# A layer of two attentions and a feed-forward: groups turned four steps ahead, feed-forward stores in two halves

## The chip, the cores and the metric

One core of a Trainium2 chip. The metric is the device time of one launch in microseconds (us); a time is the median over runs. A core has TensorE (PE, matrix products; PEld are its weight loads), VectorE (DVE), ScalarE (ACT), GpSimd (POOL), and SyncE (SP), which here only issues DMAs. Each engine takes its instructions in order and waits at semaphores for the others.

## The reference

The input x is (2, 256, 128, 128): batch, time, bands, channels, in float32. Three residual parts follow each other:

```python
xt = _ln(x, ln_t_w, ln_t_b).transpose(0, 2, 1, 3)
x = x + _mha(xt, t_wi, t_bi, t_wo, t_bo, H_T, cm).transpose(0, 2, 1, 3)   # over time, causal
xf = _ln(x, ln_f_w, ln_f_b)
x = x + _mha(xf, f_wi, f_bi, f_wo, f_bo, H_F, bm)                          # over bands, |i - j| <= 16
xn = _ln(x, ln_n_w, ln_n_b)
h = jax.nn.gelu(xn @ w1.T + b1, approximate=False)                         # 128 -> 512
x = x + (h @ w2.T + b2)                                                    # 512 -> 128
```

`_ln` is a layer norm over the channels, `_mha` an attention with four heads of 32 channels.

## The kernel before

**Groups and steps.** The work is cut into groups of 512 tokens (four tiles of 128). First come 128 groups of attention over time (`OverTime`). Then come 16 runs; a run covers 32 times of one batch and has eight groups of attention over bands (`OverBands`) and then the eight feed-forward groups of the same tokens (`FeedForward`). The loop over `n` in `BoundedPath.run` (line 1343) has one step for each group; a step does parts of several groups, so that every engine has work. In this text the band steps of a run are B1 to B8 and the feed steps F1 to F8, and a group is named like the step with its number. F1 is the step at which the code's `turn` is true.

**Order.** Every engine is wrapped in `InOrder` (line 963), which pins each instruction to the place at which the program issues it. The order of the code in `run` is thus the order on each engine. All pinned instructions carry the helper's line, L973, in the profile, so they are told apart by their tiles.

**What a group goes through.** `statistics` (line 406) takes the mean and variance on VectorE: four BN_STATS and four BN_AGGR, tiles `stats` and `mv`. `root` (line 423) makes 1/sqrt(variance + eps) on GpSimd with two instructions, tile `rstd`. `normalize` (line 457) writes `xh` on VectorE with four instructions. `turn` (line 474) transposes it in 32x32 blocks on VectorE (tile `z`) and writes it with four DMAs to a buffer in DRAM (`turned`, a pool of three). `fetch` (line 486) reads it back with one DMA as `xnT`, channels on partitions, which TensorE multiplies. The fetch of group n + 2 is issued in step n, ahead of the turn of that step.

**A band step** on VectorE: one operation that adds the band mask to the scores of the fourth head (`bank<-bank,band`), the turn of a later group, three operations that divide (`bank<-bank,r`, `u`, `oT`), and the residual sum (`x<-bank,x`). ScalarE takes exponentials into `pf`. For the other three heads GpSimd sets the weights outside the band to zero with two AFFINE_SELECTs each, six masks in a step (`first_mask`, line 843). TensorE then sums the masked weights with a matrix of ones (`sums`, line 857: `bank<-pf,ones`, one product for each head) and weighs the values (`bank<-pf,v`). The sums of a band group come in the step after its masks; those of B8 come in F1. In F1 VectorE inverts the sums of B8 by a reciprocal.

**A feed step** on TensorE: `hidden` multiplies `xnT` by w1 in four parts (`bank<-xnT,w1f`), ScalarE applies the gelu into `hT`, and `bank<-w2T_sb,hT` multiplies by w2. `divide` (line 951) adds the result on VectorE into `res` and calls `store` (line 1103), which at each second group issues four DMAs of 128 KB for the pair. `res` is a pool of two buffers of four groups each.

**How far ahead.** `turn_ahead(n)` (line 1370) normalizes and turns group n + 3. `statistics_of_feed(n)` (line 1366) takes the statistics and the root of feed group n + 4, late in step n, unless it is one of the first three of its run; those three (`early`, line 1364) are taken at the start of step n, right behind the masks of that step (line 1388). `late` (line 1449) issues the load of group n + 14, behind the turn.

Of the kernel before, what the change touches and what calls it, by code (L numbers as in the profile page):

```python
# [25 lines left out]
NT = 4  # L26
# [343 lines left out]
class Group:  # L370
# [32 lines left out]
    def bias(self):  # L403
        pass
# [147 lines left out]
    def divide(self):  # L552
        pass
# [127 lines left out]
def rows_of(h):  # L681
    return slice(h * D, (h + 1) * D)
# [9 lines left out]
class OverTime(Attention):  # L692
# [5 lines left out]
    early, late = (1, 2), (0, 3)  # L698
# [179 lines left out]

class FeedForward(Group):
    last = False  # L880

    def bias(self):
        path = self.path
# [67 lines left out]
    def divide(self):  # L951
        if self.last:
            for i in range(NT):
                dst = self.dst()[:, i]
                self.path.vector.tensor_tensor(dst, self.zps[i], dst, ALU.add)
                self.path.store_column(i)
        else:
            self.path.vector.tensor_tensor(self.dst(), self.zp, self.dst(), ALU.add)
            self.give("zp")
        self.store()  # L960


class InOrder:
# [14 lines left out]
class BoundedPath:  # L978
# [72 lines left out]
    def groups(self, x, out):  # L1051
        nc, k = self.nc, self.k
        B, T, FB, C = x.shape
        NC_T = T // P
        for b in range(B):
            for f0 in range(0, FB, GA):
                held = {}


                def load(g, f0=f0, b=b, held=held):  # L1060
                    if b == f0 == 0:
                        held["x"] = k.x0
                        return
                    if "x" not in held:
                        self.input_quad(held)
                    f = f0 + g // NC_T * NT
                    self.sync.dma_start(held["x"][rows_of(g)], self.of_times(x[b], g, slice(f, f + NT)))

                def store(g, f0=f0, b=b, held=held):
                    for i in range(NT if g % 2 else 0):  # L1070
                        f = f0 + i // NC_T * NT + g
                        self.sync.dma_start(
                            self.of_times(k.x1[b], i, slice(f - 1, f + 1)), held["res"][rows_of(i), :, g - 1 : g + 1]
                        )

                def part(name, g, i=None, a=0, held=held):
                    if name == "res" and name not in held:
                        self.quad(held, "res", 2)
                    if name == "x" and name not in held:
                        self.input_quad(held)  # L1080
                    if i is not None:
                        return self.longer(held[name], i * NT + g, a)
                    return held[name][:, :, g]

                for g in range(NT):
                    yield OverTime(self, partial(part, "x", g), partial(part, "res", g), partial(load, g), partial(store, g))
        for b in range(B):
            for r0 in range(0, T, RUN):
                run = []
                for t0 in range(r0, r0 + RUN, GB):  # L1090
                    held = {}


                    def load(g, t0=t0, b=b, held=held):
                        if g == 0:
                            self.input_quad(held)
                            self.quad(held, "x2", 2 * RUN // GB)
                        self.sync.dma_start(
                            held["x"][rows_of(g)].rearrange("q g t c -> q (g t) c"),
                            self.of_bands(k.x1[b], t0 + NT * g, NT),  # L1100
                        )

                    def store(g, t0=t0, b=b, held=held):
                        last = b == B - 1 and t0 == T - GB
                        n = 1 if last and g > 1 else 2
                        if last and g == NT - 1:
                            return
                        for i in range(NT if (g + 1) % n == 0 else 0):
                            self.sync.dma_start(
                                self.of_bands(out[b], t0 + NT * i + g + 1 - n, n),  # L1110
                                held["res"][rows_of(i), g + 1 - n : g + 1].rearrange("q g t c -> q (g t) c"),
                            )

                    def store_column(m, t0=t0, b=b, held=held):
                        to = out[b][t0 : t0 + GB].rearrange("(i g) (m q) c -> g m i q c", g=NT, q=D)
                        queue = self.scalar if m % 2 else self.sync
                        queue.dma_start(to[NT - 1, m], held["res"][:, NT - 1, m])

                    self.store_column = store_column

                    def part(name, g, i=None, a=0, held=held):
                        if name == "res" and name not in held:
                            self.quad(held, "res", 2)
                        if i is not None:
                            return self.longer(held[name], g * NT + i, a)
                        return held[name][:, g]

                    run += [(g, part, load, store) for g in range(NT)]
                for g, part, load, _ in run:
                    yield OverBands(self, partial(part, "x", g), partial(part, "x2", g), partial(load, g))  # L1130
                for g, part, _, store in run:
                    yield FeedForward(self, partial(part, "x2", g), partial(part, "res", g), None, partial(store, g))
# [210 lines left out]
    def run(self, x, out):  # L1343
        groups = list(self.groups(x, out))

        def do(n, *names):
            if 0 <= n < len(groups):
                for name in names:
                    getattr(groups[n], name)()

        def at(n, kind):
            return 0 <= n < len(groups) and isinstance(groups[n], kind)

        def do_at(n, kind, *names):
            if at(n, kind):
                do(n, *names)
# [7 lines left out]
        early = [i for i in range(3, len(groups)) if at(i, FeedForward) and at(i - 3, OverBands)]  # L1364

        def statistics_of_feed(n):
            if at(n + 4, FeedForward) and n + 4 not in early:
                do(n + 4, "statistics", "root")

        def turn_ahead(n):  # L1370
            do_at(n + 3, (OverBands, FeedForward), "normalize", "turn")

        groups[-1].last = True

# [3 lines left out]
        for n in range(len(groups) + 2):  # L1378
            feeds = [at(n - 2 + i, FeedForward) for i in range(5)]
            bands = [at(n - 2 + i, OverBands) for i in range(5)]  # L1380
            turn = feeds[2] and bands[1]
# [3 lines left out]
            if n == run0[0]:  # L1385
                self.free.sort(key=lambda i: i == self.banks["b2"])
            do(n, "first_half", "first_function", "first_mask")
            if n + 4 in early:
                do(n + 4, "statistics", "root")
            if n == 0:  # L1390
                do(3, "normalize_flat")
# [4 lines left out]
            if old is not None or new is not None:  # L1396
                time_scores(old, new)
                b = self.banks
# [48 lines left out]
            if n == 5:  # L1447
                k.late_weights()
            def late(n=n):
                do(n + 14, "load")  # L1450

            ahead = at(n, (OverBands, FeedForward))
# [3 lines left out]
            if not turn:  # L1456
                turn_ahead(n)
            if n != 1:
                do_at(n + 4, OverTime, "normalize", "turn")
            if ahead and not turn:  # L1460
                late()
# [9 lines left out]
            if not bands[2] and not turn:  # L1471
                statistics_of_feed(n)
# [26 lines left out]
            if turn:  # L1499
                turn_ahead(n)  # L1500
                late()
# [4 lines left out]
            if bands[2] or turn:  # L1506
                statistics_of_feed(n)
# [108 lines left out]
```

## Time and profile before

| what | us |
|---|---|
| median of 3 runs (2622.3 to 2624.03) | 2622.48 |
| the profiled execution, its own time | 2624.33 |
| its span, first to last instruction | 2622.3 |
| TensorE busy | 2611.9 (100%) |
| VectorE busy | 2136.2 (81%) |
| GpSimd busy | 1956.2 (75%) |
| ScalarE busy | 1824.6 (70%) |
| DMA queue 1, share of 16 engines | 50.3% |

The granted TensorE clock is 0.999 of full speed. The page gives busy time for each engine, the chain of work that ended last, and groups of equal instructions. The timeline lists instructions in order of time: start, length, engine, line, operation, out<-in, count, and in brackets the idle time before it with what ended it. The view by windows gives, for each stretch, its length and then the busy time of PE, PEld, DVE, ACT and POOL, each with the number of instructions. Ends of matmuls are modelled, so a busy TensorE is not by itself TensorE at its peak.

### The profile page before, as it was taken

The numbers are of one execution on the slowest core, as the hardware profiler recorded it, in microseconds if no ns is written. First come the engines' busy times: TensorE is split into PE (matmuls) and PEld (weight loads), VectorE is DVE, ScalarE is ACT, GpSimd is POOL, SyncE is SP. The second block draws the span as 40 slices with busy tenths as digits, with TensorE's granted clock in tenths as the row PEclk, the third lists the DMA queues.
The fourth block names the chain that finished last, engine by engine and source line by source line (L and its number), as shares of the span: only waits on it lengthen the run. The fifth ranks groups of instructions, "written<-read, shape, count | busy, mean of one in ns | idle before, by whom it ended". The sixth has DMA issues, their size and how long they took to land.

```text
span 2622.3 us, 156624 instructions
## 1 busy us (share of the span) xinstructions
PE 2611.9 (100%) x68688; PEld 1766.0 (67%) x68688; DVE 2136.2 (81%) x6410; ACT 1824.6 (70%) x3543; POOL 1956.2 (75%) x2311
## 2 busy tenths in 40 slices
PE   9999999999999999999999999999999999999999
PEld 6666666666666667666666666666666666766666
DVE  8888888888888897977878779788787797887974
ACT  7989998999899875564655746647557466475563
POOL 7999999999999987666667666665776666656762
PEclk9999999999999999999999999999999999999999
DMA  6656555565565544455455445454554444545543
GB/s 156 166 148 159 147 153 151 150 157 147 151 153 152 127 120 124 121 124 126 116 127 129 119 121 126 119 129 111 130 128 119 125 118 124 131 111 128 128 100 89
DMA packets 469798, 344.99 MB, mean 132 GB/s; under 512 B 43120, under 2 KB 404464, under 8 KB 469104
## 3 DMA queue, kind: packets, MB, share of 16 engines
q1 hardware_dynamic: 468408, 334.41, 50.3%
q8 instruction: 541, 8.86, 1.5%
q14 instruction: 153, 1.25, 0.2%
q10 hardware_dynamic: 696, 0.46, 0.1%
HBM read 167.98 MB, written 166.72 MB: 128 GB/s over the span
## 4 chain that ended last, share of the span: by engine, by line
PE 99%; DVE 0%; DMA 0%; ACT 0%; issue 0%; ACTq 0%; DVEq 0%
PE bank L973 99%; DMA x<-in_x 0%; ACT pf L973 0%; DVE stats L973 0%; DVE xnT L973 0%; ACTq L973 0%; ACT p L973 0%; DVE xh L973 0%; DVE vy L973 0%; ACT lnv L973 0%; DVE res L973 0%; DVE mv L973 0%; ACT root L973 0%; DVE rstd L973 0%; DVEq L973 0%
## 5 line engine op out<-in xcount | busy, mean ns | idle before, releaser
L973 ACT ACTIVATE hT<-bank,b 128x512 f32<-128x512 f32 x512 | 346.9, 688 | 522.5 <-PE bank L973 497.8
L973 POOL TENSOR_SCALAR_AFFINE_SELECT pf<-pf 128x512 f32<-128x512 f32 x768 | 476.6, 635 | 242.2 <-ACT pf L973 215.8
L973 PEld LDWEIGHTS bank<-w2T_sb,hT 128*32 128x32 f32 x16384 | 465.6, 110 | 137.4 <-issue 114.6
L973 PE MATMUL bank<-xnT,wf 128*32 128x512 f32 x4096 | 510.5, 593 | 1.2 <-ACT pf L973 0.7
L973 PE MATMUL bank<-xnT,w1f 128*32 128x512 f32 x4096 | 500.9, 592 | 0.0
L973 PE MATMUL bank<-w2T_sb,hT 128*32 128x128 f32 x16384 | 500.7, 273 | 0.0
L973 ACT ACTIVATE p<-bank 128x512 f32<-128x512 f32 (+1 forms) x1024 | 430.3, 495 | 63.5 <-PE bank L973 63.5
L973 DVE TENSOR_SCALAR xh<-x,mv,rstd 128x160 f32<-128x160 f32 (+1 forms) x1012 | 393.8, 432 | 35.9 <-POOL rstd L973 25.6
L973 POOL TENSOR_SCALAR_AFFINE_SELECT p<-p 128x1024 f32<-128x1024 f32 (+2 forms) x384 | 363.7, 947 | 57.3 <-ACT p L973 49.0
L973 PEld LDWEIGHTS bank<-wf,xnT 128*32 128x32 f32 x8192 | 237.5, 110 | 150.1 <-issue 91.0
L973 POOL TENSOR_TENSOR p<-p,p 128x512 f32<-128x512 f32 x256 | 323.7, 1286 | 10.7
L973 DVE BATCH_NORM_STATS2 stats<-x 128x6 f32<-128x128 f32 x1536 | 328.9, 277 | 3.1 <-DMA x<-in_x 3.1
L973 DVE TENSOR_TENSOR res<-bank,res 128x512 f32<-128x512 f32 (+1 forms) x259 | 171.0, 661 | 191.3 <-PE bank L973 163.3
L973 PE MATMUL bank<-qT,kT 32*64 32x80 f32 (+4 forms) x16384 | 303.7, 271 | 0.8 <-issue 0.7
L973 PEld LDWEIGHTS bank<-qT,kT 32*64 32x64 f32 x16384 | 260.6, 131 | 52.9 <-ACT kT L973 50.6
L973 ACT ACTIVATE pf<-bank 128x512 f32<-128x512 f32 x512 | 264.4, 603 | 35.1 <-PE bank L973 34.7
L973 DVE STREAM_TRANSPOSE z<-xh 128x512 f32<-128x512 f32 x380 | 270.4, 712 | 13.3
L973 POOL TENSOR_SCALAR rstd<-mv 128x4 f32<-128x4 f32 x251 | 57.3, 228 | 296.6 <-DVE mv L973 295.5
L973 PE MATMUL bank<-wn,oT 128*32 128x128 f32 x8192 | 276.3, 274 | 0.1
L973 POOL TENSOR_TENSOR rstd<-rstd,mhalf 128x4 f32<-128x4 f32 x251 | 260.6, 1038 | 20.9
L973 PE MATMUL bank<-wf,xnT 128*32 128x128 f32 x8192 | 272.9, 273 | 0.0
L973 DVE TENSOR_TENSOR bank<-bank,r 128x512 f32<-128x512 f32 x240 | 165.9, 691 | 108.0 <-PE bank L973 80.4
(100 smaller groups left out, 3746.2 us busy)
## 6 DMA issues: line engine op xcount, KB each, us to landing
turned<-z SPq DMA_DIRECT2D x1520, 64.0 KB, 2.6
xnT<-turned SPq DMA_DIRECT2D x380, 256.0 KB, 3.3
x<-res SPq DMA_DIRECT2D x256, 128.0 KB, 2.5
x<-x SPq DMA_DIRECT2D x128, 256.0 KB, 3.7
out<-res SPq DMA_DIRECT2D x252, 128.0 KB, 2.3
x<-in_x SPq DMA_DIRECT2D x124, 256.0 KB, 4.4
x<-in_x SPq DMA_DIRECT2D x4, 128.0 KB, 3.2
x<-in_x SPq DMA_DIRECT2D x6, 64.0 KB, 2.6
```

Source lines behind the costliest of these rows:

```text
L973: return self.tc.keep_in_program_order(emit(*args, **kwargs))
```

## The change

**Turned four steps ahead.** `turn_ahead(n)` turns group n + 4. The statistics move with it: `statistics_of_feed(n)` takes group n + 5, but not in the last band step, B8; the first three of a run are taken at the start of steps n with n + 5 among them; and F5's are taken at the start of F1. The fetch stays where it was.

**Stores in two halves.** `store` issues the first two of the four DMAs of a pair and returns the other two, which `late` issues a step later, behind that step's turn and ahead of its load. The last four groups of all are stored as before.

```diff
@@ class FeedForward, divide
-        self.store()
+        self.others = self.store()
+
+    def store_others(self):
+        if self.others is not None:
+            self.others()
@@ store of a feed group
-                        for i in range(NT if (g + 1) % n == 0 else 0):
-                            self.sync.dma_start(
-                                self.of_bands(out[b], t0 + NT * i + g + 1 - n, n),
-                                held["res"][rows_of(i), g + 1 - n : g + 1].rearrange("q g t c -> q (g t) c"),
-                            )
+                        if (g + 1) % n:
+                            return
+
+                        def some(rows):
+                            for i in rows:
+                                self.sync.dma_start(
+                                    self.of_bands(out[b], t0 + NT * i + g + 1 - n, n),
+                                    held["res"][rows_of(i), g + 1 - n : g + 1].rearrange("q g t c -> q (g t) c"),
+                                )
+
+                        some(range(NT if last else NT // 2))
+                        if not last:
+                            return partial(some, range(NT // 2, NT))
@@ run
         def statistics_of_feed(n):
-            if at(n + 4, FeedForward) and n + 4 not in early:
-                do(n + 4, "statistics", "root")
+            if n + 5 not in early and not (at(n, OverBands) and at(n + 1, FeedForward)):
+                do_at(n + 5, FeedForward, "statistics", "root")
 
         def turn_ahead(n):
-            do_at(n + 3, (OverBands, FeedForward), "normalize", "turn")
+            do_at(n + 4, (OverBands, FeedForward), "normalize", "turn")
@@ run, at the start of a step, behind first_mask
-            if n + 4 in early:
+            if n + 5 in early:
+                do(n + 5, "statistics", "root")
+            if turn:
                 do(n + 4, "statistics", "root")
@@ run, late
             def late(n=n):
+                do_at(n - 2, FeedForward, "store_others")
                 do(n + 14, "load")
```

The order of TensorE and of ScalarE, and the banks that they use, are the same in both kernels. On GpSimd, where the band steps of a run end, this stood before (`pf<-pf` are the masks, six for a step; a pair of `rstd` rows is a root):

```order
L973 AFFINE_SELECT pf<-pf 128x512 x30
L973 TENSOR_SCALAR rstd<-mv 128x4
L973 TENSOR_TENSOR rstd<-rstd,mhalf 128x4
L973 AFFINE_SELECT pf<-pf 128x512 x6
L973 TENSOR_SCALAR rstd<-mv 128x4
L973 TENSOR_TENSOR rstd<-rstd,mhalf 128x4
L973 AFFINE_SELECT pf<-pf 128x512 x6
L973 TENSOR_SCALAR rstd<-mv 128x4
L973 TENSOR_TENSOR rstd<-rstd,mhalf 128x4
L973 AFFINE_SELECT pf<-pf 128x512 x6
L973 TENSOR_SCALAR rstd<-mv 128x4
L973 TENSOR_TENSOR rstd<-rstd,mhalf 128x4
```

The x30 are the masks of B1 to B5, and the last x6 those of B8; the root behind these is that of F4. Now, at the same place:

```order
L978 TENSOR_SCALAR rstd<-mv 128x4
L978 TENSOR_TENSOR rstd<-rstd,mhalf 128x4
L978 AFFINE_SELECT pf<-pf 128x512 x6
L978 TENSOR_SCALAR rstd<-mv 128x4
L978 TENSOR_TENSOR rstd<-rstd,mhalf 128x4
L978 AFFINE_SELECT pf<-pf 128x512 x6
L978 TENSOR_SCALAR rstd<-mv 128x4
L978 TENSOR_TENSOR rstd<-rstd,mhalf 128x4
L978 AFFINE_SELECT pf<-pf 128x512 x6
L978 TENSOR_SCALAR rstd<-mv 128x4
L978 TENSOR_TENSOR rstd<-rstd,mhalf 128x4
L978 AFFINE_SELECT pf<-pf 128x512 x6
```

These are the roots of F1 to F4, each ahead of the masks of B5 to B8 (line L978 is the helper's new number). The root of F4 has moved from behind the masks of B8 to ahead of them.

VectorE from the start of B8 to the reciprocal in F1, before (`bank<-bank,band` opens a band step):

```order
L973 SCALAR_TENSOR_TENSOR bank_115<-bank_115,band 128x512
L973 TENSOR_SCALAR xh<-x_22992,mv,rstd 128x5x32 x4
L973 STREAM_TRANSPOSE z<-xh 128x512
L973 TENSOR_TENSOR bank_109<-bank_109,r_25856 128x512
L973 TENSOR_TENSOR x_23573<-bank_110,x_23573 128x512
L973 SCALAR_TENSOR_TENSOR u<-bank_109,r_25856 128x512
L973 TENSOR_TENSOR oT<-bank_114,u 128x4x4x32
L973 BN_STATS stats<-x_22992 128x6 x4
L973 BN_AGGR mv<-stats 128x2 x4
L973 RECIPROCAL ln<-bank_115 128x512
```

And now, from the end of B7:

```order
L978 BN_STATS stats<-x_23004 128x6 x4
L978 BN_AGGR mv<-stats 128x2 x4
L978 SCALAR_TENSOR_TENSOR bank_115<-bank_115,band 128x512
L978 TENSOR_SCALAR xh<-x_23004,mv,rstd 128x5x32 x4
L978 STREAM_TRANSPOSE z<-xh 128x512
L978 TENSOR_TENSOR bank_109<-bank_109,r_25881 128x512
L978 TENSOR_TENSOR x_23585<-bank_110,x_23585 128x512
L978 SCALAR_TENSOR_TENSOR u<-bank_109,r_25881 128x512
L978 TENSOR_TENSOR oT<-bank_114,u 128x4x4x32
L978 BN_STATS stats<-x_23585 128x6 x4
L978 BN_AGGR mv<-stats 128x2 x4
L978 RECIPROCAL ln<-bank_115 128x512
```

The statistics of F4 stand a step earlier, at the end of B7, and those of F5 stand where F4's were. The turn of B8 (`xh`, `z`) is now that of F4 instead of F3.

SP, in feed steps, before (`turned<-z` are the four writes of a turn):

```order
L973 DMA xnT<-turned 128x512
L973 DMA turned<-z 32x4x128 x4
L973 DMA out<-res 32x8x128 x4
L973 DMA xnT<-turned 128x512
L973 DMA turned<-z 32x4x128 x4
```

And now:

```order
L978 DMA xnT<-turned 128x512
L978 DMA turned<-z 32x4x128 x4
L978 DMA out<-res 32x8x128 x2
L978 DMA xnT<-turned 128x512
L978 DMA turned<-z 32x4x128 x4
L978 DMA out<-res 32x8x128 x2
```

Two of the four stores have moved behind the next step's turn; a `turned` row now writes the group of one step later.

More of the change, by code (lines that the diff above doesn't have):

```diff
@@ L880 @@
     last = False
+    others = None
     def bias(self):
```

## Prediction

> **What bounds the kernel now.** I read the page first, then TensorE's waits, then the span cut at the runs, then the timeline of one change from band steps to feed steps. A run is 8 band steps (B1 to B8) and 8 feed steps (F1 to F8); there are 16.
>
> ```profile
> span 2622.3 us, 156624 instructions
> ...
> PE 2611.9 (100%) x68688; PEld 1766.0 (67%) x68688; DVE 2136.2 (81%) x6410; ACT 1824.6 (70%) x3543; POOL 1956.2 (75%) x2311
> ...
> PE 99%; DVE 0%; DMA 0%; ACT 0%; issue 0%; ACTq 0%; DVEq 0%
> ```
> TensorE (PE) is busy almost without a break, and the chain that ended last is TensorE for 99%. Its waits:
>
> ```profile
> PE bank L973 <- POOL ident masks.py:199: 1.5, 1, 1.5
> PE bank L973 <- issue: 1.0, 4, 0.3
> PE bank L973 <- ACT pf L973: 0.7, 1, 0.7
> ```
> No DMA is among them, so none waited for a turned tile. A busy row alone could hide slack, so here is the span from the first feed step of the first run to that of the last, and three runs of it (length, then PE busy):
>
> ```profile
> 972.21:2557.05 1584.84, 1583.24 (x41291) 1055.87 (x41287) 1279.14 (x3857) 940.00 (x1569) 1049.79 (x1444) 1.00 0.49 122
> 1396.00:1501.26 105.26, 105.26 (x2761) 69.72 (x2757) 84.76 (x257) 62.58 (x105) 69.86 (x97) 1.00 0.49 122
> 1501.26:1606.51 105.25, 105.25 (x2761) 69.54 (x2756) 84.88 (x257) 62.48 (x105) 69.79 (x97) 1.00 0.50 125
> 1606.51:1712.65 106.14, 105.45 (x2761) 69.45 (x2756) 84.99 (x257) 62.59 (x105) 69.78 (x97) 1.00 0.47 121
> ```
> ```profile
> 1684.33 1.58 ACT pf L973 x3
> ```
> Undisturbed runs agree to 0.01 us. The third holds the chain's one long piece off TensorE, and is 0.89 longer: a wait of TensorE is not made up later. 15 runs at 105.25 are 1578.75; the stretch took 1584.84, so 6.09 us of scattered waits is all that better timing could return there. So each edit is worth what it adds to or takes from TensorE's waits.
>
> **The change part by part.** *Turned a step earlier.* The four DMAs that write a turned tile go out a step sooner, so the fetch of xnT, behind them on SP's queue, no longer stands waiting for their landing:
>
> ```profile
> SPq L973 <- DMA turned<-z: 416.0, 465, 3.7
> ```
> ```profile
> xnT<-turned SPq DMA_DIRECT2D x380, 256.0 KB, 3.3
> ```
> ```profile
> 1184.43 0.34 SPq L973 DMA_DIRECT2D xnT<-turned  x1
> ...
> 1190.55 1.90 PE L973 MATMUL bank<-xnT,w1f 128*32 128x512 f32 x16
> ```
> These 416 us are SP's own. The tile of F2 is fetched at 1184.43, lands some 3.3 later and is used at 1190.55: 2.8 to spare. Up to a step (6.1) more makes it some 9. Since TensorE never waited for a fetch, the gain is 0; the cover is needed less, not more.
>
> *Stores in halves.* 252 stores stay 252 issues of 128 KB; half are issued a step later, behind the turned tile and ahead of the next load. Nobody computes with what they write, and the result buffers are a pair, each reused a run later. I take 0, bounded below by the 6.09 above if spread stores should also quiet the scattered waits, and above by 0, since the fetches they could delay now have a step more.
>
> *Statistics a step earlier.* Counts stay the same on VectorE (DVE) and GpSimd (POOL); places change where bands turn into feed. Before, the statistics of F1, F2, F3 stand early in B5, B6, B7 and those of F4 late in B8. Now F1 to F3 stand early in B4 to B6, F4 late in B7, none in B8, and F5 early in F1. Each is followed on GpSimd by its root. GpSimd keeps the program's order, so the root of F4 now stands ahead of the six masks of B8, where before it came behind them. GpSimd there, before:
>
> ```profile
> 1176.44 3.93 POOL L973 TENSOR_SCALAR_AFFINE_SELECT pf<-pf 128x512 f32<-128x512 f32 x6 [0.97 <-ACT pf L973]
> 1180.35 0.23 POOL L973 TENSOR_SCALAR rstd<-mv 128x4 f32<-128x4 f32 x1
> 1180.66 1.04 POOL L973 TENSOR_TENSOR rstd<-rstd,mhalf 128x4 f32<-128x4 f32 x1
> 1182.67 3.93 POOL L973 TENSOR_SCALAR_AFFINE_SELECT pf<-pf 128x512 f32<-128x512 f32 x6 [0.97 <-ACT pf L973]
> 1189.25 0.23 POOL L973 TENSOR_SCALAR rstd<-mv 128x4 f32<-128x4 f32 x1 [2.65 <-DVE mv L973]
> ```
> The masks of B8 run from 1182.67 to 1186.60, gated by ScalarE. Now they wait for the root, the root for the mean and variance (mv), and those come late in VectorE's step:
>
> ```profile
> 1157.23 0.70 DVE L973 SCALAR_TENSOR_TENSOR bank<-bank,band 128x512 f32<-128x512 f32 x1 [0.50 <-PE bank L973]
> 1163.45 0.70 DVE L973 SCALAR_TENSOR_TENSOR bank<-bank,band 128x512 f32<-128x512 f32 x1 [0.50 <-PE bank L973]
> ...
> 1169.86 0.69 DVE L973 SCALAR_TENSOR_TENSOR bank<-bank,band 128x512 f32<-128x512 f32 x1
> ...
> 1176.26 0.69 DVE L973 SCALAR_TENSOR_TENSOR bank<-bank,band 128x512 f32<-128x512 f32 x1
> ...
> 1182.65 0.69 DVE L973 SCALAR_TENSOR_TENSOR bank<-bank,band 128x512 f32<-128x512 f32 x1
> 1183.25 1.60 DVE L973 TENSOR_SCALAR xh<-x,mv,rstd 128x160 f32<-128x160 f32 x4
> ...
> 1188.02 0.86 DVE L973 BATCH_NORM_STATS2 stats<-x 128x6 f32<-128x128 f32 x4
> 1188.79 0.36 DVE L973 BATCH_NORM_AGGREGATE mv<-stats 128x2 f32<-128x6 f32 x4
> ```
> The first five open B4 to B8; the turn of B8 begins at 1183.25. B4 waited for TensorE, so it starts at 1157.23 as before. A step with statistics takes 6.40 without a wait (1169.86 to 1176.26), so B5, B6, B7 open at 1163.63, 1170.03, 1176.43. B7 then has the form that B8 has now: 5.37 from 1182.65 to the late statistics at 1188.02. So those of F4 start at 1181.80 and end 1.13 later (1188.79 + 0.36 - 1188.02), at 1182.93. GpSimd answered 0.10 after such an end (1189.15 to 1189.25): 1183.03. The root takes 1.35 (1180.35 to 1181.70), the masks 3.93: from 1184.38 to 1188.31, 1.7 later than before. Who needs them:
>
> ```profile
> 1187.52 0.13 PEld L973 LDWEIGHTS bank<-pf,ones 128*32 128x32 f32 x4 [0.30 <-issue]
> 1187.95 1.04 PE L973 MATMUL bank<-pf,ones 128*32 128x512 f32 x8
> ```
> The sums over B8's weights stand in F1 and ran at 1187.95; three of their four heads wait for GpSimd, the third for the last mask. Before, 1.35 us lay between; now 0.36 are missing. The restart after a release has one row near it:
>
> ```profile
> 1180.25 0.59 ACT L973 COPY kT<-bank 128x512 f32<-128x512 f32 x1 [0.69 <-PE bank L973]
> ...
> 1180.99 0.81 PEld L973 LDWEIGHTS bank<-qT,kT 32*64 32x64 f32 x64 [0.20 <-ACT kT L973]
> ```
> 0.15 from 1180.84 to 1180.99. So the wait is 0.36 to 0.51 a run; I take 0.45, nearer the end that has a restart in it. TensorE keeps its order, so what is queued behind the sums waits too: the weighing of B8, the output of B7 and F2's first products, ready or not.
>
> The 3.93 of the masks is a span; the row behind starts 3.91 after the first. The Trainium skill (Perfetto Trace Analysis, GPSIMD Engine Instruction) says that such spans are unreliable and that the spacing of starts should be used. By that the sum is 0.02 a run less, 0.3 us in all; here the two hardly differ.
>
> *Behind it on VectorE.* The turn in B8, now of F4, waits for that root until about 1184.4, where it began at 1183.25: 1.2 later. From there to F1's reciprocal VectorE has as many operations as before (F5's statistics in the place of F4's), so it runs about 1.2 later into F1. The next that TensorE takes from it, by order of the banks, is B8's output bank:
>
> ```profile
> 1204.77 0.66 DVE L973 TENSOR_TENSOR x<-bank,x 128x512 f32<-128x512 f32 x1
> ...
> 1207.00 1.93 PE L973 MATMUL bank<-w2T_sb,hT 128*32 128x128 f32 x64
> ```
> Emptied at 1205.43, used at 1207.00: 1.57 covers 1.2, and TensorE is itself 0.45 later. Cost 0.
>
> **The sum.** 16 runs times 0.45 is 7.2 us (4.8 to 8.2 for 0.30 to 0.51, the lower end with 0.06 for small errors in eight added rows). The profiled execution took 2624.33, its span and 2.03 around it: with the change 2631.5. The median shown, 2622.48, is 1.85 below that execution; against it, 2629.7.
>
> **The rivals.** *The masks come in time* (not slower): were the root done 0.15 to 0.4 sooner, because VectorE is quicker out of B4 to B7 than its rows or the restart is shorter, 0 to 0.3 a run is left: 2622.5 to 2627.3. It decides at 0.33 a run, that is 5.2 us. For it: I add eight rows and miss by only 0.36. Against: VectorE stood saturated in the same form before, with steps of 6.39 to 6.41.
>
> *TensorE has slack.* The weight loads are 67% busy; if TensorE idled inside its rows, work behind the sums could be done faster and the delay swallowed: 2622.5. Against it stand the runs of 105.25 and the wait that lengthened one. The Trainium skill (Perfetto Trace Analysis, Identifying the Most-Contended Engine) says matmul busy time is a poor measure of distance to the roof and sends the reader to load time, which by its figure here would leave a third of the span free; the run lengths do not bear that out.
>
> *Faster.* Earlier fetches and halved stores thin out the scattered waits. At most 6.09 comes back, 2616.4, and only with no new wait; the waits that carry a name carry no DMA.
>
> *A second wait.* If VectorE is later into F1 than 2.0, the bank at 1207.00 is late as well. A further 0.4 a run gives 2636.
>
> That the change doesn't take place is excluded: the order shows the moved rows.
>
> **How the numbers follow.** The wait as worked out: 0.56, 2629.7 (own range 2627.3 to 2631.5). Masks in time: 0.32. Slack: 0.04. Faster: 0.05. Second wait: 0.03. A measurement of this kernel can tell about 0.2%, 5.2 us, from no change. Slower by more than that: 0.56 + 0.03 = 0.59; within: 0.32 + 0.04 = 0.36; faster: 0.05. The range reaches down through the cases without a wait, less the executions' own spread of some 1 us, and up to 0.51 a run with 2 us for scattered waits: 2621.5 to 2633.0.
>
> **What would show it.** In the changed profile: GpSimd's masks of B8 start some 1.7 later, right behind a root; TensorE waits once a run, at the sums in F1, for GpSimd's pf, 16 times; undisturbed runs take 105.7, not 105.25; SP's wait for turned tiles is nearly gone. I am wrong if runs stay at 105.25, or if TensorE's wait stands elsewhere.

## The result, and the profile after

The changed kernel takes 2629.84 us (median of 22 runs, 2626.89 to 2634.11), the kernel before 2622.64 us (22 runs beside them): 7.2 us more, a ratio of 1.0027 with a 95% interval of 1.0021 to 1.0032. The profiled execution of the changed kernel took 2629.27 us, 4.9 us more than that of before; its span is 2627.5 us, 5.2 more.

Three parts of the changed kernel's page: the span, the busy times, the chain that ended last by engine and by line.

```profile
span 2627.5 us, 156484 instructions
...
PE 2617.1 (100%) x68688; PEld 1862.0 (71%) x68688; DVE 2130.3 (81%) x6410; ACT 1825.3 (69%) x3543; POOL 1956.3 (74%) x2311
...
PE 98%; POOL 1%; DVE 0%; DMA 0%; issue 0%; ACT 0%; ACTq 0%; DVEq 0%
```

GpSimd (POOL) has entered the chain with 1%. All its pieces there lie between 944 and 978 us, in the first run; what the other runs lose does not show in the chain. The same number of weight loads (PEld) is busy for 96 us more than before, 71% in place of 67%; what that is comes at the end.

The span cut at the same instruction of each run, its first product with w2T. First the changed kernel (length, then TensorE's busy time, then that of the weight loads): one run, and all from the first of these products to that of the last run. Then the kernel before, one run and all.

```profile
1193.26:1298.89 105.63, 105.63 (x2758) 74.66 (x2754) 84.62 (x257) 62.65 (x105) 69.79 (x96) 1.00 0.49 123
981.53:2569.75 1588.22, 1587.70 (x41288) 1141.08 (x41284) 1272.96 (x3857) 940.76 (x1569) 1047.04 (x1440) 1.00 0.48 122
```

```profile
1403.76:1509.01 105.25, 105.25 (x2756) 69.68 (x2752) 84.88 (x257) 62.57 (x105) 69.85 (x96) 1.00 0.49 123
979.97:2564.80 1584.83, 1583.23 (x41288) 1055.55 (x41284) 1279.41 (x3857) 940.37 (x1569) 1046.91 (x1440) 1.00 0.48 122
```

An undisturbed run takes 105.63 in place of 105.25: 0.38 more, and PE shows as busy in all of it. So the wait has to be looked for elsewhere than in PE's idle time. Here is GpSimd at the end of the run whose cut lies at 1193.26; times here are 0.99 above those of the same place in the prediction's rows (its cut lies at 1192.27).

```profile
1177.43 3.93 POOL L978 TENSOR_SCALAR_AFFINE_SELECT pf<-pf 128x512 f32<-128x512 f32 x6 [0.97 <-ACT pf L978]
1183.99 0.23 POOL L978 TENSOR_SCALAR rstd<-mv 128x4 f32<-128x4 f32 x1 [2.63 <-DVE mv L978]
...
1185.32 3.93 POOL L978 TENSOR_SCALAR_AFFINE_SELECT pf<-pf 128x512 f32<-128x512 f32 x6
```

The masks of B7 end at 1181.36, GpSimd waits 2.63 for VectorE's mean and variance, does the root of F4, and only then starts the masks of B8, at 1185.32, with nothing idle between. They were held for the root, not for ScalarE's `pf` as before. VectorE and the weight loads around it:

```profile
1182.77 0.86 DVE L978 BATCH_NORM_STATS2 stats<-x 128x6 f32<-128x128 f32 x4
1183.55 0.36 DVE L978 BATCH_NORM_AGGREGATE mv<-stats 128x2 f32<-128x6 f32 x4
...
1185.38 1.61 DVE L978 TENSOR_SCALAR xh<-x,mv,rstd 128x160 f32<-128x160 f32 x4 [0.89 <-POOL rstd L978]
```

```profile
1188.51 0.12 PEld L978 LDWEIGHTS bank<-pf,ones 128*32 128x32 f32 x2 [0.30 <-issue]
1188.94 0.12 PEld L978 LDWEIGHTS bank<-pf,ones 128*32 128x32 f32 x2 [0.31 <-issue]
1189.31 0.14 PEld L978 LDWEIGHTS bank<-pf,ones 128*32 128x32 f32 x4 [0.25 <-POOL pf L978]
```

The sums of B8 (`bank<-pf,ones`): the loads of the first two heads go on time; the third's wait for the last mask, which ends at 1189.25, and the fourth's stand behind them. PE's row shows no pause there, because the products of the first two heads, and those queued behind them, stand in it.

Each of the four heads takes 32 columns of TensorE (`128*32` in the rows), so half of the columns runs on. From the first load of the sums at 1188.51 to the cut at 1193.26 are 4.75 us, as many as before (1187.52 to 1192.27). The time is lost later, at the next products of another shape: the scores of the next bands (`bank<-qT,kT`), here for the changed kernel and the one before.

```profile
1243.99 0.97 PE L978 MATMUL bank<-qT,kT 32*64 32x80 f32 x64
```

```profile
1242.62 0.97 PE L973 MATMUL bank<-qT,kT 32*64 32x80 f32 x64
```

From the cut to these are 50.73 us in place of 50.35: the 0.38 of a run.

Over the whole kernel the two views of the waits say this (us in total, times, longest):

```profile
PE bank L978 <- POOL pf L978: 0.2, 1, 0.2
```

```profile
PEld bank L978 <- POOL pf L978: 5.8, 18, 1.2
```

Of the 5.8 us, 2.1 are three waits in the first run; the others are mostly of 0.25. They tell where TensorE waits, not how much a run loses: without any wait, too, the loads of two passes stand 0.30 apart in the rows above.

SP's wait for turned tiles has fallen from 416.0 to 116.4 us, and none of it is left after 960 us, where the runs are:

```profile
SPq L978 <- DMA turned<-z: 116.4, 148, 4.2
```

TensorE never waited for these fetches within the runs, and no time came from it.

**The first run.** It loses more than the others. GpSimd there, changed, and TensorE's loads for the sums in three of its last four steps up to F1:

```profile
958.84 0.94 POOL L978 TENSOR_SCALAR w1f<-w1T_sb,cols_sb 128x256 f32<-128x256 f32 x1
...
971.03 0.23 POOL L978 TENSOR_SCALAR rstd<-mv 128x4 f32<-128x4 f32 x1 [0.90 <-DVE mv L978]
971.34 1.04 POOL L978 TENSOR_TENSOR rstd<-rstd,mhalf 128x4 f32<-128x4 f32 x1
972.36 1.29 POOL L978 TENSOR_TENSOR x<-x,orow 128x512 f32<-128x512 f32 x1
973.61 3.92 POOL L978 TENSOR_SCALAR_AFFINE_SELECT pf<-pf 128x512 f32<-128x512 f32 x6
```

```profile
956.60 0.16 PEld L978 LDWEIGHTS bank<-pf,ones 128*32 128x32 f32 x8
...
963.72 0.14 PEld L978 LDWEIGHTS bank<-pf,ones 128*32 128x32 f32 x4 [0.74 <-POOL pf L978]
...
977.59 0.11 PEld L978 LDWEIGHTS bank<-pf,ones 128*32 128x32 f32 x2 [1.16 <-POOL pf L978]
```

And the sums of before, at the first and the last of these four steps:

```profile
957.12 0.16 PEld L973 LDWEIGHTS bank<-pf,ones 128*32 128x32 f32 x8
...
976.02 0.14 PEld L973 LDWEIGHTS bank<-pf,ones 128*32 128x32 f32 x4 [0.26 <-POOL pf L973]
```

In this run alone GpSimd adds the output's bias row between the masks (`x<-x,orow`, 1.29 a step; for the other runs it does so in the feed steps ahead of their bands), and folds w1 there (`w1f`, 0.94 twice). Already before it had no time left: TensorE's loads waited 0.26 for it at the sums of F1. From the sums at 957.12 to the cut at 979.97 are 22.85 us before; from 956.60 to 981.53, 24.93 in the changed kernel: 2.08 more, not 0.38. Behind this cut nothing is added: it is 51.19 us to the next `qT,kT` in both, since half of the columns was late here already before.

So the profiled executions add up: 2.08 in the first run, 15 times 0.38 = 5.7 in the others, together 7.8. Against it stand scattered waits, fewer in this one execution: 1588.22 less 15 times 105.63 is 3.77, where before had 6.08 in the same stretch (1584.83 less 15 times 105.25); with 0.52 less ahead of the first run's changeover and 0.25 more behind the last, that makes the 5.2 between the spans.

### The profile page after: what moved, and what is told of

The parts are those of the page before. It is cut to its first block, busy times and chain, and to the rows that moved or that the text cites. A ratio compares the mean times of both kernels' runs of the same rounds, so it can differ in the third digit from the quotient of the medians.

```text
span 2627.5 us, 156484 instructions
## 1 busy us (share of the span) xinstructions
PE 2617.1 (100%) x68688; PEld 1862.0 (71%) x68688; DVE 2130.3 (81%) x6410; ACT 1825.3 (69%) x3543; POOL 1956.3 (74%) x2311
## 4 chain that ended last, share of the span: by engine, by line
PE 98%; POOL 1%; DVE 0%; DMA 0%; issue 0%; ACT 0%; ACTq 0%; DVEq 0%
PE bank L978 98%; POOL pf L978 1%; DMA xnT<-turned 0%; POOL rstd L978 0%; POOL x L978 0%; DMA x<-in_x 0%; DVE xh L978 0%; POOL w1f L978 0%; DVE stats L978 0%; DVE xnT L978 0%; DVE oT L978 0%; DVE bank L978 0%; DVE u L978 0%; ACT pf L978 0%; DVE x L978 0%
## 5 line engine op out<-in xcount | busy, mean ns | idle before, releaser
L978 ACT ACTIVATE hT<-bank,b 128x512 f32<-128x512 f32 x512 | 346.7, 687 | 527.0 <-PE bank L978 500.5
L978 POOL TENSOR_SCALAR_AFFINE_SELECT pf<-pf 128x512 f32<-128x512 f32 x768 | 476.6, 635 | 206.7 <-ACT pf L978 180.4
L978 PEld LDWEIGHTS bank<-w2T_sb,hT 128*32 128x32 f32 x16384 | 531.8, 110 | 81.1 <-issue 59.8
L978 PE MATMUL bank<-xnT,w1f 128*32 128x512 f32 x4096 | 570.9, 592 | 0.0
L978 PE MATMUL bank<-w2T_sb,hT 128*32 128x128 f32 x16384 | 561.9, 273 | 0.0
L978 PE MATMUL bank<-xnT,wf 128*32 128x512 f32 x4096 | 516.7, 593 | 1.0 <-DVE xnT L978 0.5
L978 ACT ACTIVATE p<-bank 128x512 f32<-128x512 f32 (+1 forms) x1024 | 430.3, 495 | 62.9 <-PE bank L978 62.9
L978 DVE TENSOR_SCALAR xh<-x,mv,rstd 128x160 f32<-128x160 f32 (+1 forms) x1012 | 393.0, 431 | 48.9 <-POOL rstd L978 39.7
L978 POOL TENSOR_SCALAR_AFFINE_SELECT p<-p 128x1024 f32<-128x1024 f32 (+2 forms) x384 | 363.7, 947 | 56.8 <-ACT p L978 48.5
L978 PEld LDWEIGHTS bank<-wf,xnT 128*32 128x32 f32 x8192 | 242.0, 110 | 146.6 <-issue 86.0
L978 DVE TENSOR_TENSOR res<-bank,res 128x512 f32<-128x512 f32 (+1 forms) x259 | 170.8, 660 | 202.1 <-PE bank L978 183.6
L978 POOL TENSOR_TENSOR p<-p,p 128x512 f32<-128x512 f32 x256 | 323.8, 1286 | 10.7
L978 DVE BATCH_NORM_STATS2 stats<-x 128x6 f32<-128x128 f32 x1536 | 329.0, 277 | 3.3 <-DMA x<-in_x 3.3
L978 POOL TENSOR_SCALAR rstd<-mv 128x4 f32<-128x4 f32 x251 | 57.3, 228 | 335.0 <-DVE mv L978 334.2
L978 PE MATMUL bank<-qT,kT 32*64 32x80 f32 (+4 forms) x16384 | 302.7, 271 | 0.5 <-issue 0.4
L978 PEld LDWEIGHTS bank<-qT,kT 32*64 32x64 f32 x16384 | 260.3, 131 | 52.1 <-ACT kT L978 50.6
L978 ACT ACTIVATE pf<-bank 128x512 f32<-128x512 f32 x512 | 265.1, 603 | 34.7 <-PE bank L978 34.5
L978 PE MATMUL bank<-wn,oT 128*32 128x128 f32 x8192 | 285.7, 274 | 0.1
L978 DVE STREAM_TRANSPOSE z<-xh 128x512 f32<-128x512 f32 x380 | 270.4, 712 | 13.7
L978 PE MATMUL bank<-wf,xnT 128*32 128x128 f32 x8192 | 277.6, 273 | 0.0
L978 POOL TENSOR_TENSOR rstd<-rstd,mhalf 128x4 f32<-128x4 f32 x251 | 260.7, 1038 | 20.9
L978 PEld LDWEIGHTS bank<-xnT,w1f 128*32 128x32 f32 x4096 | 189.1, 110 | 120.4 <-issue 103.7
```

Source lines behind the costliest of these rows:

```text
L978: return self.tc.keep_in_program_order(emit(*args, **kwargs))
```

## The experiments

Each set of runs has runs of the kernel before on the same chip beside it: median 2624.67 in the first set (four kernels), 2623.58 in the second (three). A root is the pair of GpSimd rows that makes `rstd`.

### F4's statistics early

```diff
-        early = [i for i in range(3, len(groups)) if at(i, FeedForward) and at(i - 3, OverBands)]
+        early = [i for i in range(4, len(groups)) if at(i, FeedForward) and at(i - 4, OverBands)]
```

> The changed kernel, with the statistics and the root of F4 early in B7, right behind the masks of B7, as those of F1 to F3 stand in B4 to B6; turn and halved stores stay as changed. Theory (the root of F4, fed late in B7, holds back the masks of B8): the root is done by about 1.3 us after the masks of B7, long before ScalarE hands over B8, so the 0.38 us of each run go: undisturbed runs 105.25, and 2622.6 us for the kernel, up to 2624.7 if the first run keeps what it lost beyond that. Rival 1 (the turn a step earlier costs it, on VectorE or SP) and rival 2 (the halved stores cost it): nothing that they name is undone, so runs stay at 105.63 and the time at 2629.8.

Measured: 2625.09 us (11 runs), ratio to before 1.0006, 0.9996 to 1.0015. Its GpSimd in B7 and B8, and one run:

```profile
1175.24 3.94 POOL L978 TENSOR_SCALAR_AFFINE_SELECT pf<-pf 128x512 f32<-128x512 f32 x6 [0.95 <-ACT pf L978]
1179.16 0.23 POOL L978 TENSOR_SCALAR rstd<-mv 128x4 f32<-128x4 f32 x1
...
1181.47 3.94 POOL L978 TENSOR_SCALAR_AFFINE_SELECT pf<-pf 128x512 f32<-128x512 f32 x6 [0.95 <-ACT pf L978]
```

```profile
1191.06:1296.30 105.24, 105.24 (x2756) 69.41 (x2752) 84.55 (x257) 62.71 (x105) 69.98 (x96) 1.00 0.49 123
```

The root still stands ahead of the masks of B8, but runs at once behind those of B7, and the masks wait for ScalarE again. Runs are back at 105.24 with the turn a step earlier and the stores in halves. So, by the length of a run, neither of these costs anything, and neither brings anything. The cause lies in where the statistics of one group stand.

### The statistics alone

```diff
-            if at(n + 4, FeedForward) and n + 4 not in early:
-                do(n + 4, "statistics", "root")
+            if n + 5 not in early and not (at(n, OverBands) and at(n + 1, FeedForward)):
+                do_at(n + 5, FeedForward, "statistics", "root")
...
-            if n + 4 in early:
+            if n + 5 in early:
+                do(n + 5, "statistics", "root")
+            if turn:
                 do(n + 4, "statistics", "root")
```

(on the kernel before)

> The kernel before, with only the statistics and roots of the feed groups a step earlier, as the change has them; the turn stays three steps ahead and the stores stay whole. Theory: the same root stands ahead of the masks of B8, so runs of 105.63 and 2629.8 us. Rivals 1 and 2 (turn, stores): none of theirs is in it, 105.25 and 2622.6.

Measured: 2629.30 us, ratio 1.0021, 1.0012 to 1.0030. One run, and its weight loads' wait:

```profile
1512.02:1617.65 105.63, 105.63 (x2758) 80.01 (x2754) 84.65 (x257) 62.54 (x105) 69.75 (x96) 1.00 0.49 123
```

```profile
PEld bank L973 <- POOL pf L973: 5.9, 18, 1.1
```

The moved statistics make the whole 0.38 a run without the rest of the change, with 5.9 us in 18 waits, as in the changed kernel.

### Stores whole

```diff
-                        some(range(NT if last else NT // 2))
-                        if not last:
-                            return partial(some, range(NT // 2, NT))
+                        some(range(NT))
```

> The changed kernel, with the pairs stored whole again. Theory and rival 1: 105.63 a run and 2629.8 us, as with halves. Rival 2 (the halved stores): 105.25 and 2622.6.

Measured: 2629.81 us, ratio 1.0021, 1.0012 to 1.0030; a quiet run takes 105.66. The halves are no part of it.

### One more power behind the root

```diff
     def root(self, again=False):
...
         gpsimd.tensor_tensor(self.rstd, self.rstd, path.k.mhalf, ALU.pow)
+        if again:
+            spare = path.small.tile([P, NT], F32, name="spare", bufs=2)
+            gpsimd.tensor_tensor(spare, self.mv[:, :, 1], path.k.mhalf, ALU.pow)
...
-                do_at(n + 5, FeedForward, "statistics", "root")
+                do_at(n + 5, FeedForward, "statistics")
+                if at(n + 5, FeedForward):
+                    groups[n + 5].root(again=at(n + 1, OverBands))
```

> The changed kernel, with one more GpSimd power of 1.04 us into a spare tile behind the root of F4 in each run, that is between the root and the masks of B8; nobody reads it. Theory: the masks of B8 end 1.0 later and TensorE's wait grows one for one, 0.38 to 1.4 a run: undisturbed runs 106.65, and 2629.8 + 16 times 1.02 = 2646 us. Rival 3 (not the masks, but the turn of F4, which waits on VectorE for the same root and makes VectorE late, sets the wait): rstd is there before the added power starts, so runs stay at 105.63 and the time at 2629.8. Rival 4 (TensorE has slack inside its rows and swallows part of a delay): clearly less than 1.0 a run.

Measured: 2645.94 us (2644.81 to 2646.71), ratio 1.0082, 1.0069 to 1.0096. GpSimd, VectorE's turn of F4, and a run:

```profile
1189.57 1.01 POOL L981 TENSOR_TENSOR spare<-mv,mhalf 128x4 f32<-128x4 f32 x1
1190.54 3.94 POOL L981 TENSOR_SCALAR_AFFINE_SELECT pf<-pf 128x512 f32<-128x512 f32 x6
```

```profile
1189.63 1.61 DVE L981 TENSOR_SCALAR xh<-x,mv,rstd 128x160 f32<-128x160 f32 x4 [0.89 <-POOL rstd L981]
```

```profile
1519.02:1625.64 106.62, 106.61 (x2759) 80.50 (x2754) 84.76 (x257) 62.70 (x105) 70.91 (x97) 1.00 0.48 122
```

The row takes 0.97 by the spacing of starts, and a run grows by 0.99 (106.62 less 105.63). VectorE's turn waits 0.89, just as without the added row, so it is the masks that set TensorE's wait and not the turn. TensorE gave back nothing of 0.99 a run. The weight loads speak to a rule of the Trainium skill (Perfetto Trace Analysis, Identifying the Most-Contended Engine), that load time tells more of the headroom of TensorE than the busy time of products: at 67% the loads seemed to leave a third free, and none of it took up this delay.

### The statistics of F4 ahead of the division

```diff
+            ahead_of_division = bands[2] and feeds[4]
+            if ahead_of_division:
+                statistics_of_feed(n)
...
-            if bands[2] or turn:
+            if (bands[2] or turn) and not ahead_of_division:
                 statistics_of_feed(n)
```

> The changed kernel, with the late statistics of F4 in B7 moved four VectorE rows ahead, in front of the division by B6's sums (some 2.5 us sooner); the root stays ahead of the masks of B8, in the same place on GpSimd. Theory (not the place of the root alone, but the late end of what feeds it): the root ends by 1183 in the changed kernel's times in place of 1185.3, before ScalarE hands over B8 at about 1183.7; the wait is gone, runs 105.25 and 2622.6 to 2624.7 us, unless the division, 1.1 us later, makes TensorE wait in its turn. Rival (a root ahead of the masks costs its own 1.3 us wherever its statistics stand): runs stay at 105.63, 2629.8 us.

Measured: 2624.83 us, ratio 1.0008, 0.9999 to 1.0017. GpSimd between the masks of B7 and those of B8, and a run:

```profile
1180.08 0.23 POOL L978 TENSOR_SCALAR rstd<-mv 128x4 f32<-128x4 f32 x1
...
1182.27 3.93 POOL L978 TENSOR_SCALAR_AFFINE_SELECT pf<-pf 128x512 f32<-128x512 f32 x6 [0.84 <-ACT pf L978]
```

```profile
1191.87:1297.12 105.25, 105.25 (x2757) 69.44 (x2753) 84.53 (x257) 62.65 (x105) 69.84 (x96) 1.00 0.50 123
```

GpSimd's order is that of the changed kernel, and the wait is gone. The root ahead of the masks costs nothing by itself; it costs when VectorE's statistics, which feed it, come after ScalarE's weights. No other wait took its place.

### The foldings out of GpSimd's full steps

```diff
-            if n in run0[3:5]:
-                self.fold_first(n - run0[3])
+            if n in run0[0:2]:
+                self.fold_first(n - run0[0])
```

(on the kernel with F4's statistics early)

> As the kernel with F4 early, and besides the two foldings of w1f on GpSimd (0.94 us each) stand in B1 and B2 of the first run, where GpSimd idles over 1 us a step, in place of B4 and B5. Theory (the first run loses more than the others, 2.1 us to the changed kernel and 1.2 to F4 early, since GpSimd there also carries the bias rows and these foldings and has no time left): the first change loses nothing against the kernel before, 1.2 us less than F4 early, that is some 2623.5 to 2624 us beside 2624.67 for the kernel before and 2625.09 for F4 early; in the profile the first feed step stands where that of the kernel before does, within 0.3 us, once delays ahead of the first run's bands are taken off. Rival (the first run loses to VectorE, not GpSimd): still 1.2 behind.

Measured: 2624.25 us, ratio 1.0004, 0.9995 to 1.0013. Sums of the first run and its cut, for F4 early (three and two steps ahead of F1) and for this kernel (three and two steps ahead, and in F1):

```profile
955.47 0.16 PEld L978 LDWEIGHTS bank<-pf,ones 128*32 128x32 f32 x8
...
962.64 0.14 PEld L978 LDWEIGHTS bank<-pf,ones 128*32 128x32 f32 x4 [0.80 <-POOL pf L978]
```

```profile
979.58:2563.70 1584.12, 1583.69 (x41288) 1071.53 (x41284) 1272.96 (x3857) 942.20 (x1569) 1049.77 (x1440) 1.00 0.49 122
```

```profile
958.27 0.16 PEld L978 LDWEIGHTS bank<-pf,ones 128*32 128x32 f32 x8
964.50 0.16 PEld L978 LDWEIGHTS bank<-pf,ones 128*32 128x32 f32 x8
...
976.37 0.56 PEld L978 LDWEIGHTS bank<-pf,ones 128*32 128x32 f32 x8 [0.30 <-issue]
```

```profile
981.12:2564.17 1583.05, 1582.49 (x41286) 1068.98 (x41282) 1272.81 (x3857) 941.56 (x1569) 1048.34 (x1440) 1.00 0.49 122
```

From the sums to the cut, F4 early took 979.58 less 955.47 = 24.11, 1.26 above the 22.85 of before; this one takes 981.12 less 958.27 = 22.85, and no load waits for GpSimd. So the first run's further loss was GpSimd's. Of the 2.08, F4's late statistics are 0.82, which F4 early took away; the other 1.26 come with one more root, of some 1.3, ahead of the masks of B8 on a GpSimd that had no pause left. Behind the cut it is now 50.80 us to the next `qT,kT` in place of 51.19: the wait of the kernel before is gone too. The whole time was expected 0.7 to 1.2 us below the kernel before and came out 0.67 above; 11 runs cannot tell so little.

### The halves alone

The kernel before, with `store`, `store_others` and the call in `late()` of the change.

> The kernel before, with the stores in halves alone. Theory: nothing, 105.25 a run and 2624.7 us within 1 us; scattered waits as before. Rival (halved stores thin out the scattered waits): up to 6 us less.

Measured: 2623.29 us beside 2623.58, ratio 1.0004, 0.9995 to 1.0013. Runs of 105.24 to 105.26 where nothing else waited. From cut to cut all 15 runs took 1583.46, so scattered waits of 1583.46 less 15 times 105.25 = 4.7 us; 6.08 before, 5.4 with F4 early. Nothing that one execution could tell from before.

## Why the prediction was right

**The place and the chain of causes** were as foretold up to the sums. Brought to the times of before (0.99 off), F4's statistics started at 1181.78 (1181.80 worked out), GpSimd answered at 1183.00 (1183.03), the masks began at 1184.33 (1184.38), and VectorE's turn at 1184.39 (1184.4). Two experiments hold the cause: the statistics alone bring all of it, and the same order on GpSimd without the late feed brings none.

**The size per run** was taken at 0.45 and came out at 0.38. The masks were 1.66 late (1184.33 less 1182.67) where 1.7 was worked out, and the restart after the release, for which the 0.15 of another row was allowed, was 0.06 (from the last mask's end at 1189.25 to the load at 1189.31). The upper bound of 0.51 carried a restart more than twice as long as the one seen.

**All of TensorE waits in F1, ready or not**: that is not what the rows show. Two of the four heads' columns ran on, nothing was lost between the sums and the cut, and the 0.38 came out some 50 us later, when the next products of another shape needed the late columns as well (50.73 in place of 50.35). The size is what it would have been, since the late half sets the time; the place and the manner are not.

**Sixteen equal runs** is the step that failed. I read one changeover and multiplied. The first run's GpSimd carries rows between its masks that no other run has there, and the new places of the statistics cost 2.08 in it, 0.82 for F4's and 1.26 for one root more on a full engine. Too much per run (16 times 0.07) and too little for the first run (1.7) came near to cancelling, so the total of 7.2 is better than its parts: the parts measured make 15 times 0.38 and 2.08, 7.8. That the forecast of 2629.7 lies so near to 2629.84 is in part luck.

**One for one** held, up to 0.99 a run more. A wait that comes ahead of the sums isn't simply added, though. This run of the kernel with one more power held a late load of F1's products, for which no other engine is named:

```profile
1511.56 0.16 PEld L981 LDWEIGHTS bank<-xnT,w1f 128*32 128x32 f32 x7 [0.70 <-issue]
```

```profile
1412.36:1519.02 106.66, 106.66 (x2759) 75.95 (x2754) 84.80 (x257) 62.95 (x105) 70.98 (x97) 1.00 0.49 122
```

It is 0.04 longer than the undisturbed 106.62: its sums came later to masks that were late anyway. That would make a kernel with a regular wait less sensitive to scattered ones, and may be why the loss is 7.2 us in the first comparison and 4.6 to 5.1 for the two like kernels beside a before of 2624.67; but the intervals of these ratios overlap, so there may be no difference to explain. It is read from one run and was not tested by itself.

**Turn, halves, second wait** at 0 were right. The turned tiles left SP's waits in the runs without a gain. B8's output bank was emptied at 1207.54, used at 1207.98:

```profile
1206.89 0.65 DVE L978 TENSOR_TENSOR x<-bank,x 128x512 f32<-128x512 f32 x1
```

```profile
1207.98 1.99 PE L978 MATMUL bank<-w2T_sb,hT 128*32 128x128 f32 x58
```

1.13 later than before, as worked out (1.2), with 0.44 of the cover left.

**What would show it**: the masks behind a root and the run length showed as said. "TensorE waits once a run" did not show in PE's waits, where one of 0.2 stands, but in those of its weight loads.

**Left open**: what sets the scattered waits of some 4 to 6 us in each execution. They are not all scattered: 0.84 of them stand behind the first run's cut (51.19 us to the next `qT,kT`, where an undisturbed run has 50.35) in the kernel before, with the halves alone and with F4 early, and 0.45 with the foldings moved (50.80). No version tried is faster than the kernel before; with the wait taken out, the change leaves the time where it was.

## What to carry to other kernels

When work is issued earlier, follow each of its small instructions on the engine that keeps order: the power of 1 us was harmless behind the masks and harmless early ahead of them, and cost only where it waited for a late producer with the critical engine's input queued behind it. Such a root goes right behind work whose end is already past its producer. And before a loss is multiplied by its repeats, look at the first repeat by itself: set-up work there may have used up the margin.

## What the runs showed of the hardware

Half of TensorE's columns can run ahead of the other half. After the sums in F1, where two of four products waited, the loads of two following products alternate, and still do so 50 us later, at the end of the feed steps (weight loads of the changed kernel):

```profile
1239.89 0.23 PEld L978 LDWEIGHTS bank<-w2T_sb,hT 128*32 128x32 f32 x4
1240.01 0.15 PEld L978 LDWEIGHTS bank<-xnT,w1f 128*32 128x32 f32 x4
1240.11 0.23 PEld L978 LDWEIGHTS bank<-w2T_sb,hT 128*32 128x32 f32 x4
...
1243.98 0.81 PEld L978 LDWEIGHTS bank<-qT,kT 32*64 32x64 f32 x64 [0.20 <-ACT kT L978]
1244.88 0.16 PEld L978 LDWEIGHTS bank<-xnT,wf 128*32 128x32 f32 x8
```

They come in one piece again only behind the products of another shape (32\*64). The Trainium skill (TensorEngine Tiling (Array Packing), Key Properties) says that tiles work independently and that a change of tiling drains TensorE; both agree with these rows. The lead saved no time: the next product of the other shape came 0.38 later, with the late half. Nor did it grow with a later mask: with one more power behind the root it is again 50.73 us from the cut to that product, and the further 0.99 us lie between the sums and the cut. But it lengthens the loads' rows: 74.66 us in a run in place of 69.68. So a higher busy share of loads (71%, not 67%) stood here for a slower kernel with the same loads.
